# Layer 1 of a two-layer graph kernel: where X W is computed, the order of the loop head, and the broadcast of the weights

## The chip, the cores and the metric

The kernel runs on one core of a Trainium2 chip, in float32 throughout. The metric is the device time of one execution in microseconds (us); the runs shown are summed up by their median. A profile comes from one execution of its own, and its times are counted from that execution's first instruction.

## The reference, cut to what matters

There are N = 2708 nodes with 128 features; `adj` is a 2708 x 2708 matrix of zeros and ones. Layer 0 mixes neighbours and normalizes. Layer 1 is the part that the change is about:

```python
XW = X @ W                                  # 2708 x 128
s_col = XW @ a[0, :128]
s_row = XW @ a[0, 128:]
den = exp(leaky_relu(s_row[:, None] + s_col[None, :], 0.01))
num = A @ den
att = where(num != 0, den / num, 0)
H = A @ (att @ XW)
x = layernorm(X + H)
```

## The kernel before

**How layer 1 is computed.** exp(leaky(r + c)) is one of two exponentials, by the sign of r + c. So the kernel sorts the nodes into 24 groups of at most 126 by their row score and by their column score. A running sum over the groups then gives `num` with one matmul for each group and strip, where the plain way takes a product over all nodes. For this it needs the sorted order as tables of row numbers, and it gathers the rows of `adj_t` (its columns sorted by row score) and of XW (sorted by column score) with indirect DMAs.

**Stages, in order of time.**

1. Attention of layer 0, up to about 217 us.
2. Diffusion of layer 0 (lines 865 to 925). Six strips of 512 nodes (the last has 148), each 44 matmul instructions into `dif_acc`. After strip s come its normalized rows, turned (`x1_in_sbuf`, line 807, into tile `x1_t`), its scores (`scores`, `tally`, `picked`), and in strips 0 to 3 also X W of the strip (`projected`, line 848: four blocks, eight matmul instructions into `xw_ps`), copied by VectorE (line 887) and stored to the DRAM tensor `xw_d` through ScalarE's DMA queue (`store_xw`, line 857).
3. From line 897 on, the order on each engine is written out by hand: `mm`, `dve`, `act` and `gps` pin every instruction behind the one traced before it on the same engine (line 172). Strips 4 and 5 end here; their X W is done at lines 943 to 946, after the counts.
4. The look-up of interval ends (lines 984 to 1018). From the counts of nodes below each of 256 bounds the kernel follows, for 11 steps on VectorE, "the farthest bound that a group can reach" (line 988), and turns the ends into thresholds `thr`.
5. The tables (lines 1147 to 1241). Row scores (k) and column scores (j) are compared with `thr`, numbered, and placed with one-hot matmuls. The k tables give `k_no` (row numbers for `gather`), the j tables `j_no` (for `gather_xw`) and the sorted column scores `j_t`.
6. The loop over 24 groups (line 1340), a pipeline of three stages: step g multiplies group g (`multiply`, PE then a copy to `q`), divides group g-1 (`divide` on VectorE, `power` on ScalarE), weighs group g-2 with its XW rows (`weigh`, PE, into `m_acc`). ScalarE takes a logarithm and an exponential of each group, and loads a function table before each.
7. The last product with `adj_t` and the layer norm, from about 620 us.

**Fillers.** Sums over all rows that the groups start from (`tot`) are spread over stages 3 to 5 as jobs. An "e" job loads 128 rows of `adj_t` (768 KB, `first_strips`, line 691, a tile of pool `nat`) on SyncE's queue and sums them in eight small matmuls; a "k" job (`kept_strips`, line 707) sums rows that are in SBUF already, in twelve. `fill("eke")` puts three such jobs at this place of TensorE's order. There are 13 "e" and 22 "k" jobs left for `fill`.

**What the change and the prediction touch besides.** `att` (line 295, 22 blocks of 512 bytes per partition) is layer 0's attention term, last read by `mixed` in stage 3. Its pool `lp` is closed at line 950; the pools `tab` and `tmp` of stages 4 and 5 take over its memory. A new tile in memory taken over waits until the accesses to the old tile there have ended, DMAs among them. `ring[0]` is the memory of `x_sb`. `later_weights` (line 1258), called in step 0 of the loop, spreads the sorted column scores of groups 1 to 3 with matmuls, writes exp of all of them to the DRAM tensor `g_d`, and reads them back to all partitions with two broadcasting DMAs into `wt` (groups 4 to 7, then 8 to 23). `weights(g)` on ScalarE turns them into the weights of group g; it must be done before `multiply(g)`. `helped` (line 1291) names the two copies of step 0 that ScalarE makes instead of VectorE.

Of the kernel before, what the change touches and what calls it, by code (L numbers as in the profile page):

```python
# [45 lines left out]
def grouped(  # L46
# [602 lines left out]
    nat = pool("nat", 3, stack=l0)  # L649
# [157 lines left out]
    def x1_in_sbuf(s, tp):  # L807
        nb = blocks(s)
        x1_t = work2.tile([P, SW], F32, tag="x1_t", name="x1_t")
        dve(  # L810
            "tensor_copy", x1_t[:, : nb * P], tp[:, :nb, :].rearrange("p b i -> p (b i)")
        )
        return x1_t
# [34 lines left out]
    def projected(s, x1_t):  # L848
        pn = ps_mm.tile([P, SW // P, D], F32, tag="mm", name="xw_ps")
        for b in range(blocks(s)):  # L850
            mm(
                nc.tensor.matmul, pn[:, b, :], x1_t[:, ts(b, P)], w_sb,
                start=True, stop=True,
            )
        return pn

    def store_xw(s, xw, nb):
        nc.scalar.dma_start(
            xw_d[s * SW : s * SW + nb * P, :].rearrange("(b p) d -> p b d", p=P), xw
        )  # L860
# [4 lines left out]
    for s in range(NS - 2):  # L865
# [20 lines left out]
        xw = work2.tile([P, 4, D], F32, tag="xw", name="xw")  # L886
        nc.vector.tensor_copy(xw, projected(s, x1_t))
        store_xw(s, xw, nb)
# [24 lines left out]
    shared_row(s, row_s)  # L913
    fill("eke")
# [17 lines left out]
    shared_row(t, row_t)  # L932
    picked(t, col_t, sc_p)
# [4 lines left out]
    limited(s * 4, NB)  # L938
    picked(s, col_s, sc_p)
    act("activation", reach_b[64:], can[64:], AF.Copy, scale=-1.0, bias=Q + 1.0)  # L940
    dve("tensor_copy", reach_b[:64], reach_ps[:64, :Q])
    e2(s * 4, NB)
    xw = nat.tile([P, 6, D], F32, tag="xw_last", name="xw", bufs=1)
    act("copy", xw[:, :4, :], projected(s, x1_s))
    act("copy", xw[:, 4:, :], projected(t, x1_t)[:, :2, :])
    store_xw(s, xw, 6)
    fill("ekekek")
# [20 lines left out]
    vk = tmp.tile([P, NB], F32, name="vk")  # L968
    dve("scalar_tensor_tensor", vk, sr_p, -1.0, pad, ALU.mult, ALU.add)
    vj = tmp.tile([P, NB], F32, name="vj")  # L970
    dve("tensor_tensor", vj, sc_p, pad, ALU.add)
    back = tab.tile([P, NB], F32, name="back")
    dve("tensor_tensor", back, live, e2_p, ALU.mult)
# [13 lines left out]
    dve("tensor_copy", ends[64:, 0:1], reach_b[64:, Q - 1 :])  # L987
    for g in range(1, half_g):
        junk = tmp.tile([P, Q], F32, tag="more", name="junk")
        dve(  # L990
            "scalar_tensor_tensor", junk, bound_no, ends[:, g - 1 : g], reach_b,
            ALU.is_equal, ALU.mult, accum_out=ends[:, g : g + 1],
        )
    both = tmp.tile([P, NG - 1], F32, name="both")
    dve("tensor_scalar", both[:, : half_g - 1], ends[:, : half_g - 1], row0, None, ALU.mult)
    dve("tensor_scalar", both[:, half_g - 1 :], ends, half_on, None, ALU.mult)
    ends_ps = ps_x.tile([P, SW], F32, tag="ahead", name="ends_ps", bufs=2)
# [12 lines left out]
    fill("ekekk")  # L1010
# [90 lines left out]
    def table(name, onp, v, o, p0, between):  # L1101

        t = tmp.tile([P, 1, P], F32, name=f"{name}_t{v}")
# [27 lines left out]
    def gather_xw(g):  # L1131
# [5 lines left out]
            in_offset=bass.IndirectOffsetOnAxis(ap=j_no[:, g : g + 1], axis=0),  # L1137
# [3 lines left out]


    cs_p = tmp.tile([P, NB], F32, name="cs_p")
    dve("tensor_scalar", cs_p, sc_p, LIMIT, -LIMIT, ALU.min, ALU.max)
    dve("tensor_scalar", cs_p, cs_p, 1.0 - LEAK, None, ALU.mult)
# [6 lines left out]
    fill("kekekekek")  # L1152
# [4 lines left out]
    k_tab = table("k", k_onp, 0, *banks("x"), P - G, lambda: fill("kk"))  # L1157
    valued("k", 1, k_hot, low, 17)
    valued("j", 1, j_hot, cs_p, 0, 12)
    j_run, j_ahead, j_of = numbered("j", j_hot)  # L1160
    k_no = rows_of_table("k", k_tab, G)
    valued_by_dve("j", 0, j_hot, from_n)
    k_tab = table("k", k_onp, 1, *banks("x"), 0, lambda: fill("kkk"))
    valued("j", 1, j_hot, cs_p, 12)
    fill("k")
# [32 lines left out]
    gather(1)  # L1198
    wt = ring_p.tile([P, NG, P], F32, name="wt")
# [3 lines left out]
    carry_in(0, (0, 1), by_act)  # L1203

# [29 lines left out]
    j_tab = selected("j", j_t, [0, 1])  # L1234
    carry_in(0, (2, 3), by_dve)
    c_s = tab.tile([P, NG], F32, name="c_s")
    j_no = rows_of_table("j", j_tab, P)
    dve("tensor_copy", c_s, j_tab[:, 1, :])
    nc_s = tab.tile([P, NG], F32, name="nc_s")
    dve("tensor_scalar", nc_s, c_s, -1.0, None, ALU.mult)  # L1240
    carry_in(1, (0, 1), by_act)
    carry_in(1, (2, 3), by_dve)
    tots.close()
# [9 lines left out]
    gather_xw(0)  # L1253
    gather(2)
    gather_xw(1)
    gather(3)

    def later_weights():

        o = ps_num.tile([P, SW], F32, tag="num", name="c_ps")  # L1260
        for g in range(1, 4):
            spread_c(o[:, ts(g - 1, P)], g)
        mm(
            nc.tensor.matmul, o[:NG, 3 * P :], four[:, :NG], j_t[:, 1, :],
            start=True, stop=True,
        )
        g_r = tab.tile([P, P], F32, name="g_r")
        act("activation", g_r[:NG], o[:NG, 3 * P :], AF.Exp)
        nc.sync.dma_start(g_d, g_r[:NG, P - G :])
        act(  # L1270
            "activation", gb[:, 1:, :],
            o[:, : 3 * P].rearrange("p (g c) -> p g c", g=3)[:, :, P - G :], AF.Exp,
        )
        for g in range(1, 4):
            weights(g, gb[:, g, :])
        for g0, g1 in ((4, 8), (8, NG)):
            nc.sync.dma_start(
# [62 lines left out]
    for step in range(NG + LAG):  # L1340
# [17 lines left out]
        if g < NG:  # L1358
            for i0, i1 in parts_m:
                log(g, i0, i1)  # L1360
# [553 lines left out]
```

## Time and profile before

| what | value |
|---|---|
| runs shown | 739.69, 739.81, 743.85 us; median 739.81 us |
| the profiled execution's own time | 739.68 us |
| its span, first to last instruction | 737.9 us |
| mean granted TensorE clock | 0.982 of full speed |
| TensorE, VectorE, ScalarE, GpSimd busy | 708.7, 443.8, 419.5, 233.9 us |
| data moved by DMA | 179.89 MB, mean 244 GB/s |

The profiled execution takes 1.8 us more than its span; its time is 0.13 us from the median. Three kinds of answer are used below. A timeline lists instructions by start time with, in square brackets, how long the engine had been idle before and which instruction or DMA released it. A table of stretches gives each engine's busy time in a stretch with the number of its instructions, then the granted clock, the busy share of the DMA engines, and GB/s. The list of DMA issues gives the size of each and the time from issue to landing. PE is TensorE, PEld its weight loads, DVE VectorE, ACT ScalarE, POOL GpSimd, SP SyncE.

### The profile page before, as it was taken

The page shows a single profiled execution, that of the slowest core. Times are in us where ns is not written, and L with a number is a line of the kernel's source. Part 1 is how long each engine was busy: PE and PEld are TensorE (multiplying, and loading weights), DVE is VectorE, ACT ScalarE, POOL GpSimd, SP SyncE. Part 2 cuts the span into 40 slices and gives each one's busy share as a digit, 9 for nine tenths or more (in the row PEclk, how much of TensorE's full clock was granted, in tenths as well). Part 3 has the DMA queues.
Part 4 walks back from the last instruction along what each step waited for, and adds up shares of the span by engine and source line. Part 5 has one row for each costly group of instructions (what it writes and reads, how often), then busy time and mean ns, then how long its engine had stood idle before and what let it go on. Part 6 is the DMA issues. An engine that isn't in the chain of part 4 may idle for free. (4 is left out here: it accounts for less than half of the span.)

```text
span 737.9 us, 7958 instructions
## 1 busy us (share of the span) xinstructions
PE 708.7 (96%) x2639; PEld 358.8 (49%) x2639; DVE 443.8 (60%) x925; ACT 419.5 (57%) x601; POOL 233.9 (32%) x240
## 2 busy tenths in 40 slices
PE   7999999999999999999798899999999999999995
PEld 4454444545464444445565344444444446444444
DVE  5676857566541452344787879999999984103032
ACT  4757867778741121211176899999999994001000
POOL 5868788879841000000004222222222300000000
PEclk9999999999979999999989999999999999999999
DMA  8868999988999998731847994444444531999970
GB/s 287 314 226 300 325 326 338 336 316 299 301 365 400 364 395 301 288 143 33 286 143 251 230 222 149 167 173 171 165 158 155 165 133 42 298 311 309 313 228 24
DMA packets 69827, 179.89 MB, mean 244 GB/s; under 512 B 6798, under 2 KB 20914, under 8 KB 66754
## 3 DMA queue, kind: packets, MB, share of 16 engines
q1 hardware_dynamic: 57188, 133.32, 52.4%
q0 software_dynamic: 6336, 43.08, 17.7%
q10 hardware_dynamic: 6254, 2.90, 1.4%
q8 instruction: 23, 0.38, 0.2%
q14 instruction: 26, 0.21, 0.1%
HBM read 176.44 MB, written 2.84 MB: 243 GB/s over the span
## 5 line engine op out<-in xcount | busy, mean ns | idle before, releaser
L201 POOL TENSOR_TENSOR total<-total,p_t 128x512 f32<-128x512 f32 (+3 forms) x111 | 124.5, 1122 | 38.3 <-ACT p_t L195 32.8
L176 PE MATMUL m_acc<-q,xws 128*128 128x512 f32 x240 | 122.2, 597 | 0.0
L176 PE MATMUL num<-ring,wt 128*128 128x512 f32 x216 | 98.8, 550 | 4.4 <-DVE q L176 3.3
L190 DVE SCALAR_TENSOR_TENSOR p_t<-sim,gentle,piece 128x512 f32<-128x512 f32 (+1 forms) x111 | 72.2, 670 | 48.5 <-PE sim L185 37.8
L185 PE MATMUL att_acc<-p_t,x_sb 128*128 128x512 f32 (+1 forms) x228 | 97.6, 555 | 2.0 <-ACT p_t L195 1.8
L185 PE MATMUL dif_acc<-strip,x_sb 128*128 128x512 f32 x220 | 98.4, 594 | 0.0
L195 ACT ACTIVATE p_t<-p_t,shift 128x512 f32<-128x512 f32 (+1 forms) x111 | 69.4, 655 | 35.0 <-DVE p_t L190 29.6
L176 DVE SCALAR_TENSOR_TENSOR q<-sr_b,nc_s,q 128x1536 f32<-128x1536 f32 (+1 forms) x48 | 77.8, 1623 | 17.8 <-ACT q L176 17.6
L176 DVE COPY q<-num 128x512 f32<-128x512 f32 (+1 forms) x142 | 83.9, 612 | 4.4 <-PE num L176 4.2
L176 PEld LDWEIGHTS m_acc<-q,xws 128*128 128x128 f32 x240 | 45.9, 192 | 56.9 <-issue 56.7
L1451 PE MATMUL h_acc<-ring,m_sb 128*128 128x512 f32 x164 | 72.3, 593 | 0.0
L176 ACT ACTIVATE q<-q,head,rest 128x1536 f32<-128x1536 f32 (+1 forms) x48 | 70.2, 1508 | 1.2 <-DVE ring L176 0.9
L176 ACT ACT_TABLE_LOAD x52 | 66.7, 1283 | 3.8 <-issue 2.9
L176 PEld LDWEIGHTS num<-ring,wt 128*128 128x128 f32 x216 | 39.4, 191 | 49.2 <-issue 34.2
L176 ACT ACTIVATE q<-q,c_s 128x1536 f32<-128x1536 f32 (+1 forms) x48 | 62.9, 1355 | 0.4
L185 PEld LDWEIGHTS att_acc<-p_t,x_sb 128*128 128x128 f32 x228 | 40.9, 202 | 45.0 <-ACT p_t L195 25.0
L185 PEld LDWEIGHTS dif_acc<-strip,x_sb 128*128 128x128 f32 x220 | 40.5, 190 | 45.8 <-issue 45.8
L176 ACT ACTIVATE row<-row 128x1354 f32<-128x1354 f32 x44 | 58.2, 1323 | 7.5 <-DMA row<-in_adj 7.5
L1461 ACT COPY ht<-h_acc 128x512 f32<-128x512 f32 (+1 forms) x6 | 3.2, 535 | 91.3 <-PE h_acc L1451 91.2
L1466 DVE TENSOR_TENSOR hh<-rows,x 128x512 f32<-128x512 f32 (+1 forms) x6 | 3.8, 641 | 84.1 <-PE rows L1385 81.7
L176 POOL DMA_INDIRECT ring<-in_adj_t,k_no x18 | 21.1, 1170 | 100.3 <-PE num L176 97.2
L1451 PEld LDWEIGHTS h_acc<-ring,m_sb 128*128 128x128 f32 x164 | 30.8, 190 | 36.8 <-issue 36.8
(289 smaller groups left out, 907.8 us busy)
## 6 DMA issues: line engine op xcount, KB each, us to landing
row<-in_adj SPq DMA_DIRECT2D x44, 677.0 KB, 5.4
strip<-in_adj_t SPq DMA_DIRECT2D x10, 2816.0 KB, 19.3
piece<-in_adj_t SPq DMA_DIRECT2D x24, 1024.0 KB, 7.0
ring<-in_adj_t SPq DMA_DIRECT2D x20, 1024.0 KB, 5.0
nat<-in_adj_t SPq DMA_DIRECT2D x13, 768.0 KB, 4.5
x_sb<-in_adj_t SPq DMA_DIRECT2D x7, 1024.0 KB, 5.0
nat<-in_adj_t POOLq DMA_DIRECT2D x9, 768.0 KB, 9.8
piece<-in_adj_t SPq DMA_DIRECT2D x7, 512.0 KB, 6.6
```

The costliest lines, as they stand in the source:

```text
L176: latest[engine] = op(*args, **kwargs)
L185: op(*args, **kwargs)
L190: return getattr(nc.vector, op)(*args, **kwargs)
L195: return getattr(nc.scalar, op)(*args, **kwargs)
L201: getattr(nc.gpsimd, op)(*args, **kwargs)
L1451: nc.tensor.matmul(acc[:, : h1 - h0], m_sb[:, kb + b, :], a[:, b, h0:h1], start=(kb + b == 0), stop=(kb + b == NB - 1),)
L1461: nc.scalar.copy(ht[:, h0:h1], acc[:, : h1 - h0])
L1466: nc.vector.tensor_tensor(hh[:, b0 : b0 + n, :], rows[:, :n, :], x1[:, ib + b0 : ib + b0 + n, :], ALU.add)
```

## The change

It has seven parts.

1. **X W moves.** The four `projected` calls of strips 0 to 3, their VectorE copies and stores leave the diffusion. `x1_in_sbuf` now keeps the turned rows of every strip in `att` in place of a tile `x1_t`. After the counts, `project` makes X W of all six strips from there, ScalarE copies it back into the same place, and two DMAs store it (blocks 0 to 11 after strip 2, blocks 12 to 21 at the end).
2. **Order before the look-up.** `vk`, `vj`, `cs_p` and `back` are computed behind the 11 steps instead of before them; `limited` and `e2` of the last strips come after the third `project`. `shared_row(s, ...)` of strip 4 goes from before the second `tally` to behind strip 5's.
3. **Fillers in another order**, with "e" jobs earlier and "k" jobs later, and a fourth buffer for the pool `nat`. To have room, `junk` of the look-up is put into `x_sb`, the two tiles `k_t` share one place, and `x1_t`, `xw` and `xw_last` are gone.
4. **Tables.** `valued_by_dve("j", 0, ...)` comes before `k_no`; four "k" jobs stand before the j tables, where there was one.
5. **Before the loop.** `gather(2)` directly follows `gather(1)`. The four `carry_in` pairs come before the j tables' matmuls. What `later_weights` did with matmuls, exponentials, the write of `g_d` and the broadcast of groups 4 to 7 now comes ahead of the loop; the broadcast of groups 8 to 23 is written at the end of step 1.
6. **In step 0.** The selection of `j_no` and `c_s` (`numbers`) and the first two `gather_xw` come after the second multiply. `weights(1)`, `weights(2)` and the two halves of the logarithm are interleaved with the multiplies; ScalarE makes the copies of strips 1 and 4 instead of 1 and 3. `weights(3)` comes after step 1's logarithm.
7. **In step 2** `weigh(0, ...)` stands before the multiply of each strip instead of after it.

```diff
-    nat = pool("nat", 3, stack=l0)
+    nat = pool("nat", 4, stack=l0)
...
-        x1_t = work2.tile([P, SW], F32, tag="x1_t", name="x1_t")
+        x1_t = att[:, s * 4 : s * 4 + nb, :].rearrange("p b i -> p (b i)")
...
+    def project(s):
+        mine = att[:, s * 4 : s * 4 + blocks(s), :]
         pn = ps_mm.tile([P, SW // P, D], F32, tag="mm", name="xw_ps")
         for b in range(blocks(s)):
             mm(
+                nc.tensor.matmul, pn[:, b, :], mine[:, b, :], w_sb, start=True, stop=True
+            )
+        act("copy", mine, pn[:, : blocks(s), :])
...
-        xw = work2.tile([P, 4, D], F32, tag="xw", name="xw")
-        nc.vector.tensor_copy(xw, projected(s, x1_t))
-        store_xw(s, xw, nb)
...
-    shared_row(s, row_s)
-    fill("eke")
+    fill("eeke")
...
     shared_row(t, row_t)
+    shared_row(s, row_s)
...
-    limited(s * 4, NB)
+    act("activation", reach_b[64:], can[64:], AF.Copy, scale=-1.0, bias=Q + 1.0)
     picked(s, col_s, sc_p)
-    act("activation", reach_b[64:], can[64:], AF.Copy, scale=-1.0, bias=Q + 1.0)
     dve("tensor_copy", reach_b[:64], reach_ps[:64, :Q])
-    e2(s * 4, NB)
-    xw = nat.tile([P, 6, D], F32, tag="xw_last", name="xw", bufs=1)
-    act("copy", xw[:, :4, :], projected(s, x1_s))
-    act("copy", xw[:, 4:, :], projected(t, x1_t)[:, :2, :])
-    store_xw(s, xw, 6)
-    fill("ekekek")
+    for n in range(NS):
+        project(n)
+        if n == 2:
+            store_xw(0, 3)
+            limited(s * 4, NB)
+            e2(s * 4, NB)
+    store_xw(3, NS)
+    fill("e")
...
-    fill("ekekk")
+    fill("ekekek")
+    back = tab.tile([P, NB], F32, name="back")
+    dve("tensor_tensor", back, live, e2_p, ALU.mult)
...
-    fill("kekekekek")
+    fill("kkekkekke")
...
-    k_tab = table("k", k_onp, 0, *banks("x"), P - G, lambda: fill("kk"))
+    k_tab = table("k", k_onp, 0, *banks("x"), P - G, lambda: fill("k"))
...
+    valued_by_dve("j", 0, j_hot, from_n)
     k_no = rows_of_table("k", k_tab, G)
-    valued_by_dve("j", 0, j_hot, from_n)
-    k_tab = table("k", k_onp, 1, *banks("x"), 0, lambda: fill("kkk"))
+    k_tab = table("k", k_onp, 1, *banks("x"), 0, lambda: fill("kekk"))
     valued("j", 1, j_hot, cs_p, 12)
-    fill("k")
+    fill("kkkk")
...
+    def spread_out_weights(g0, g1):
+        nc.sync.dma_start(
+            wt[:, g0:g1, P - G :],
+            g_d[g0:g1, :].unsqueeze(0).to_broadcast([P, g1 - g0, G]),
+        )
+
+    spread_out_weights(4, 8)
...
+            if first == 0 and s < NS - 1:
+                weigh(first, *item)
             if g < NG:
                 multiply(g, *item)
                 if (g, s) == (0, 1):
-                    later_weights()
+                    j_no.append(numbers())
+                    gather_xw(0)
+                    gather(3)
+                    gather_xw(1)
+                if (g, s) == (0, 4):
+                    weights(2, gb[:, 2, :])
                 if item[2] == half or s == NS - 1:
                     carry(g, *parts_m[s // 3])
+                    if g == 0:
+                        if s < 3:
+                            weights(1, gb[:, 1, :])
+                        log(0, *parts_m[s // 3])
...
+        if step == 1:
+            spread_out_weights(8, NG)
```

## The prediction

> **What bounds the kernel now.** I read the timeline of each stage first, then the table of stretches for the clock, then the list of DMA issues. The sum is made against the profiled execution's 739.68 us (span 737.9 us and 1.78 us around it), which is 0.13 us below the median of the runs.
>
> In the diffusion (217 to 344 us) the timeline shows TensorE without a pause: whatever is issued there moves the end. X W of strip 0 stands between two runs of `dif_acc`:
>
> ```profile
> 250.48 1.05 PE L185 MATMUL xw_ps<-w_sb,x_t 128*128 128x128 f32 x8
> 251.37 1.02 PE L185 MATMUL dif_acc<-strip,x_sb 128*128 128x512 f32 x2
> ```
>
> Its slot is the distance of the starts, 251.37 - 250.48 = 0.89 us.
>
> Between 347 and 395 us VectorE carries a chain, with waits of its own. The brackets name what ended each:
>
> ```profile
> 348.58 0.75 DVE L176 TENSOR_SCALAR_CACHE_REDUCE junk<-sb_ps,ntheta 128x512 f32<-128x512 f32 x1 [0.85 <-ACT sr_b L176]
> ...
> 360.00 0.18 DVE L176 TENSOR_TENSOR back<-live,e_p 128x22 f32<-128x22 f32 x1 [1.52 <-ACT e_p L176]
> ...
> 369.40 0.17 DVE L176 COPY thr<-thr_ps 128x11 f32<-128x11 f32 x1 [1.60 <-PE thr_ps L176]
> ...
> 374.37 0.70 DVE L176 TENSOR_TENSOR k_run<-k_run,ahead 128x528 f32<-128x528 f32 x1 [0.84 <-PE ahead L176]
> ```
>
> TensorE is nearly idle during the look-up and pays for it. These stretches (TensorE's busy time first, then five columns with the clock after them) are the 3.4 us before each of two drops, and the drops:
>
> ```profile
> 362.60:366.00 3.40, 0.34 (x11) 0.15 (x2) 3.19 (x13) 0.00 (x0) 0.00 (x0) 1.00 1.03 363
> 366.00:372.80 6.80, 6.15 (x46) 3.88 (x50) 4.28 (x14) 1.38 (x6) 0.00 (x0) 0.50 0.61 214
> 386.50:389.90 3.40, 1.76 (x39) 1.27 (x33) 3.30 (x3) 3.39 (x16) 1.60 (x1) 1.00 0.87 293
> 389.90:393.30 3.40, 3.40 (x74) 3.34 (x68) 1.62 (x5) 0.29 (x1) 0.54 (x1) 0.50 0.76 268
> ```
>
> In the group loop ScalarE has no gap once it runs: its weights of successive groups start at 434.71 and 443.57, 8.86 us for a step. So a delay at the head is kept to the end. In step 2 it does stand still:
>
> ```profile
> 421.84 1.36 ACT L176 ACTIVATE q<-q,head,rest 128x1172 f32<-128x1172 f32 x1 [0.89 <-DVE ring L176]
> 425.85 0.49 ACT L176 ACTIVATE wt<-wt,kt 128x126 f32<-128x126 f32 x1 [2.65 <-DMA wt<-g_d]
> ```
>
> The list of issues has the DMA behind that wait, and the stores of X W:
>
> ```profile
> wt<-g_d SPq DMA_DIRECT2D x1, 1008.0 KB, 37.3
> ...
> xw_d<-xw ACTq DMA_DIRECT2D x4, 256.0 KB, 7.6
> ...
> xw_d<-xw ACTq DMA_DIRECT2D x1, 384.0 KB, 8.3
> ...
> wt<-g_d SPq DMA_DIRECT2D x1, 252.0 KB, 20.3
> ```
>
> **The change, part by part.** Clock times from here on are those of the profile before, so that shifts can be read against its rows.
>
> *Diffusion.* Four slots of 0.89 us go: **-3.56 us**. Strips 3 and 4 are issued 29 us before TensorE reads them and take 19.3 us at the median, so the loads stay hidden. VectorE's copies (4 x 0.69 us) lay beside TensorE and bring nothing.
>
> *Second tally.* It waited 0.85 us for ScalarE's copy of the same bank, which now comes later. The added "e" job costs TensorE about 0.6 us ahead of `x_ps` (two jobs start at 346.61 and 347.28, 0.67 us apart), which falls into its idle 1.34 us. Of the 0.85 I take **-0.7 us**.
>
> *Look-up.* `back` waited 1.52 us for `e_p`. Without it the steps start when ScalarE's half of `reach_b` is there, 358.45, and end at 364.9, where they ended at 366.50: 1.6 us earlier. Beside them TensorE now has X W of 22 blocks. Twelve instructions took 1.50 us, so 44 take 5.5 us, from 358.0. They are paced by ScalarE: copies of 0.585 us, two PSUM buffers, and in the middle the store's issue of 0.36 us, the table load of 1.28 and the exponential of 0.21. Strip 5 then ends at 364.9, the "e" job at 365.5, so `ends_ps` starts 0.6 us after VectorE is ready. But the clock should now stand at full: twelve small matmuls that took 1.20 us at 367.18 took 0.68 at 359.97, and `thr` follows `ends_ps` by about 1.6 us instead of 2.75. `thr` is there at 367.1 where it was at 369.4: 2.3 us.
>
> *Tables.* The three "e" and three "k" jobs behind `thr_ps` take 3.4 us warm (five took 4.6 us cold), so `ahead` is ready at 371.1 and the wait of 0.84 goes: 3.2 us. `valued_by_dve` (1.14 us) fills the wait of 1.30 us that `k_no` had, so the j chain gains another 0.9: its one-hots end at 386.7, not at 390.88. The j matmuls, 4.5 us at half clock, follow at full clock behind four "k" jobs of about 0.5 us, which end at 386.1. The first `num` starts near 390.5 where it started at 395.32: **4.8 us** at best. The earlier "e" jobs find their loads landed, because the fourth buffer takes one more into the idle queue at 315 to 347 us; `gather(0)` is issued at 381 and lands before 388.
>
> *What that gives back.* `j_gt` and the placing tiles lie in the memory of `att`, which the second store still reads. VectorE meets `j_gt` at 370.4; queued behind it are `k_run` and with it both tables. The store (640 KB) is issued at 365.9. Alone, the quickest store landed 2.3 us after issue for 256 KB; beside three loads 384 KB took 8.3. The wait lies between 0 (landing by 370.4) and 3.8 us (landing after 8.3, at 374.2). It has two or three 768 KB loads beside it, fewer than the row of 8.3 had queued ahead, so I take landing at 371.7 with **+0.6 us** after the slack behind `k_of` (0.7 us). Here the Trainium skill, "DMA: Bandwidth & Descriptors", section "Issuing engines are not separate DMA queues", speaks against the change: a store from ScalarE's queue shares the same 16 engines with SyncE's loads, and only the issue is saved. By the rule at its strictest, with the four later loads (3.1 MB at about 310 GB/s, 10 us) all served before it, the wait is 8 us, and the sum below becomes 737; by the rows, where 512-byte packets came through in 8.3 us between three loads, it is under 3.8. I take the rows.
>
> So the first multiply gains 4.8 - 0.6 - 0.3 (`num` may wait for ScalarE's reading of `c_ps` in the same bank, 0 to 0.75 us) = **-3.9 us**.
>
> *Clock.* "TensorE: Matmul & The Clock Gate", section "Why this matters for your kernels", says that gaps under about 3 us between bursts are safe. The rows disagree: the stretch from 386.5 had 1.76 us of work in 3.40 and no gap over 1.6 us (387.94 to 389.54), and the clock still halved. By the rule, the 1.4 us that X W waits for ScalarE's table load is harmless. By the row it is close: a stretch with that gap holds 2.0 of 3.4 us. I take the clock as kept, and carry the other outcome as a rival.
>
> *Loop head.* In order of ScalarE: copy, weights, table load, then the first half of the logarithm as soon as three strips are copied. VectorE's `carry` ends 5.0 us after the first multiply; the logarithm started 6.8 us after it before. But the second half now stands behind a copy of 0.58 and weights of 0.42 us, and the exponential behind VectorE's `divide`: its last part ends 14.3 us after the first multiply, before 14.0. Nothing gained, 0.3 us lost. The gain is in the broadcast. `g_r` is made at the first multiply, not 3.0 us after it, so the DMA lands 3 to 4 us earlier against the loop: the 2.65 us wait goes, or shrinks to 0.5. The wait of 0.89 us for `carry` may stay. Bounds: 0 (the gathers, two of them now earlier, hold the small packets as long as they did) to -3.5; I take **-2.2 us**, with the 0.3 in it. `weigh(0)` ahead of the multiplies in step 2 needs the exponential at 12.4 us and XW rows gathered from 3.5 us on, which take 6.0 us: nothing.
>
> *Sum.* -3.56 - 0.7 - 3.9 - 2.2 = -10.36; 739.68 - 10.36 = **729.3 us**, 729.4 beside the median. The loop of 8.86 us a step and the last product are only shifted.
>
> **The rivals.**
>
> *The clock falls again* (0.16). For it: the row of 1.76 us. At half clock the six fillers take 6 us, not 3.4, `thr` is 0.6 us later, and `ahead` comes near 373.6: the tables gain about 0.7 us instead of 3.9. 739.68 - 3.56 - 0.7 - 0.7 - 2.2 = **732.5 us**.
>
> *The broadcast is no earlier and the store holds `j_gt`* (0.13). For it: 20.3 us with gathers beside it, and gathers are as many as before. Head 0 and 2.5 us more of wait: 739.68 - 3.56 - 0.7 - 1.4 = **734.0 us**.
>
> *Slower: the second store starves* (0.10). Its 512-byte packets are like the 504-byte packets of the broadcasts, which landed after 20.3 and 37.3 us beside large transfers. If the store takes 20.3 us it lands at 386.2, `j_gt` stands still for 15.8 us, and VectorE's whole order with it; less 0.6 taken already: 729.3 + 15.2 = **744.5 us**. It decides from a landing 16 us after issue. Against it: five stores took at most 8.3 us.
>
> **How the numbers follow.** The forecast of 729.3 has a chance of 0.61, with a range of its own of 727 to 731.5; the rivals 0.16, 0.13 and 0.10. About 1%, 7.4 us, is what a measurement of this kernel can tell from no change; that line is 732.4. Below it lie the forecast and, of the first rival, which is at the line, about a third: 0.66. Over 1% slower is only the third: 0.10. Same: 0.24. From 726.5 to 735.0 us lie the forecast with its bounds and the first two rivals; 2 in 10 are left for the third and for tails.
>
> **What would show it.** `dif_acc` of strip 4 ending 3.5 us earlier; no wait of VectorE for `e_p`; `thr` about 6.5 us earlier on the clock; no drop of the clock between `ends_ps` and the j tables; `j_gt` with a wait for a DMA under 1.5 us; the first `num` near 387; ScalarE's wait for `wt` under 0.6 us. It is wrong if `j_gt` waits for the store by over 4 us, if the clock halves in the look-up, or if the diffusion does not shorten.

## The result and the profile after

The changed kernel takes **729.49 us** at the median of four runs (729.12 to 731.68), beside 739.75 us for the kernel before (739.14 to 743.85, four runs): a ratio of 0.9857, 95% interval 0.9824 to 0.9889. The profiled execution took 729.28 us, its span is 727.5 us, and the mean granted clock 0.989.

The attention stage, which the change does not touch, ends between 215.6 and 221.4 us in the profiles of this study. So stages are compared by the distance between two marks, and the total from the start of the diffusion on. Each column is read from one execution:

| stretch (us) | before | after | difference | forecast |
|---|---|---|---|---|
| start of the diffusion to the last strip's first `dif_acc` | 119.89 | 116.32 | -3.57 | -3.56 |
| from there to the counts `ct` | 15.89 | 14.98 | -0.91 | -0.7 |
| `ct` to the first `num` | 42.19 | 39.00 | -3.19 | -3.9 |
| first `num` to the logarithm of step 3 | 36.56 | 32.82 | -3.74 | -2.2 |
| that logarithm to the last one | 176.72 | 176.73 | +0.01 | 0 |
| last logarithm to the end | 129.28 | 129.56 | +0.28 | 0 |
| from the start of the diffusion to the end | 520.54 | 509.41 | -11.13 | -10.36 |

The spans differ by 10.4 us, since the diffusion of the profile after happens to start 0.73 us later. The first four rows, which are the terms that the prediction priced, come to -11.41.

*Diffusion*, the timeline of TensorE: sixteen matmul instructions of a strip follow each other with nothing between them.

```profile
249.49 7.03 PE L185 MATMUL dif_acc<-strip,x_sb 128*128 128x512 f32 x16
```

*Look-up and tables*, TensorE and then VectorE. X W runs beside VectorE's steps; the 0.84 us is its wait for ScalarE, which loads a table between two copies, and `ends_ps` starts as soon as VectorE's `both` is there (360.98 us):

```profile
354.11 4.72 PE L176 MATMUL xw_ps<-w_sb,att 128*128 128x128 f32 x40
359.67 0.71 PE L176 MATMUL xw_ps<-w_sb,att 128*128 128x128 f32 x4 [0.84 <-ACT att L176]
360.31 0.85 PE L176 MATMUL tot<-nat,e_w 128*32 128x384 f32 x8
361.09 0.40 PE L176 MATMUL ends_ps<-both,ones 128*128 128x23 f32 x2
```

```profile
362.72 0.17 DVE L176 COPY thr<-thr_ps 128x11 f32<-128x11 f32 x1 [0.59 <-PE thr_ps L176]
...
365.94 0.19 DVE L176 COPY k_of<-k_run 128x24 f32<-128x24 f32 x1
367.25 0.73 DVE L176 TENSOR_TENSOR j_gt<-vj,thr 128x550 f32<-128x550 f32 x1 [1.13 <-ACT k_ons L176]
367.90 0.70 DVE L176 TENSOR_TENSOR k_run<-k_run,ahead 128x528 f32<-128x528 f32 x1
```

The wait for `thr` shrank from 1.60 to 0.59 us. `j_gt` has a new wait of 1.13 us. The profile names ScalarE's `k_ons`, but these instructions had begun at 364.71 and run on without a break to 373.97; the experiments show that it is the store.

The table of stretches has the clock at full (1.00) where it had halved:

```profile
358.40:361.80 3.40, 2.56 (x27) 1.58 (x28) 3.14 (x18) 2.07 (x5) 1.20 (x5) 1.00 0.73 233
...
382.40:385.80 3.40, 2.77 (x95) 2.50 (x85) 2.43 (x8) 1.91 (x6) 2.15 (x2) 1.00 0.59 183
385.80:389.20 3.40, 2.51 (x12) 1.65 (x13) 1.07 (x3) 1.52 (x5) 0.00 (x0) 1.00 0.99 366
```

*Before the first multiply*, TensorE, first in the kernel before and then in the changed one. `c_ps` now stands ahead of `num`, which waits for ScalarE's reading of it, and `gb_ps` waits for `j_t`:

```profile
389.54 4.48 PE L176 MATMUL tab_ps<-j_onp,j_ons 128*32 128x128 f32 x88 [1.59 <-DVE j_onp L176]
393.95 0.49 PE L176 MATMUL gb_ps<-j_t,four 128*128 128x128 f32 x2
394.41 0.63 PE L176 MATMUL j_sel<-four,j_t 128*128 128x24 f32 x4
395.32 1.99 PE L176 MATMUL num<-x_sb,wt 128*128 128x512 f32 x4 [0.29 <-ACT wt L176]
```

```profile
382.36 2.81 PE L176 MATMUL tab_ps<-j_onp,j_ons 128*32 128x128 f32 x88
385.97 0.49 PE L176 MATMUL gb_ps<-j_t,four 128*128 128x128 f32 x2 [0.80 <-ACT j_t L176]
386.39 1.26 PE L176 MATMUL c_ps<-j_t,four 128*24 128x128 f32 x8
388.37 1.98 PE L176 MATMUL num<-x_sb,wt 128*128 128x512 f32 x4 [0.72 <-ACT gb L176]
```

ScalarE copies `j_t` late because two of the `carry_in` copies, which the change moved forward, stand ahead of it:

```profile
384.83 0.80 ACT L176 COPY x_sb<-tot 2x293 f32<-2x293 f32 x2 [1.21 <-DVE x_sb L176]
385.65 0.27 ACT L176 COPY j_t<-tab_ps 128x128 f32<-128x128 f32 x1
```

*Loop head*, ScalarE in step 2: neither the stall of 0.89 us inside the logarithm nor the 2.65 us before the weights of group 4 (at 415.17) is left. The list of issues has the broadcast behind it, which took 20.3 us before, and the first store:

```profile
412.34 2.92 ACT L176 ACTIVATE q<-q,head,rest 128x1536 f32<-128x1536 f32 x2
415.17 0.48 ACT L176 ACTIVATE wt<-wt,kt 128x126 f32<-128x126 f32 x1
```

```profile
xw_d<-att ACTq DMA_DIRECT2D x1, 768.0 KB, 4.1
...
wt<-g_d SPq DMA_DIRECT2D x1, 252.0 KB, 13.9
```

### The profile page after: what moved, and what is told of

It is laid out like the page before. It is cut to its first block, busy times and chain, and to the rows that moved or that the text cites. A ratio compares the mean times of both kernels' runs of the same rounds, so it can differ in the third digit from the quotient of the medians.

```text
span 727.5 us, 7944 instructions
## 1 busy us (share of the span) xinstructions
PE 702.9 (97%) x2639; PEld 354.5 (49%) x2639; DVE 440.1 (61%) x921; ACT 421.0 (58%) x605; POOL 233.2 (32%) x240
```

## The experiments

Intervals of the ratios are about 0.3 to 0.5% to each side, 2 to 4 us, which is as much as most single parts are worth. So the ratio says where a kernel stands, and the marks in the traces say which part did it. The marks of a kernel come from one execution, which can lie off its median: by +2.8 us of 740.2 for the kernel before with the broadcast early, and by +1.6 us of 736.6 for the changed kernel with `gather(2)` in the loop. The loop's head scatters most, so a difference of 1 us there in a single row proves little. In the table, "dif" is the first stretch of the table above, "tables" runs from `ct` to the first `num`, "head" from there to the logarithm of step 3, "rest" from the start of the diffusion to the end.

| kernel | ratio to before, interval | dif | tables | head | rest |
|---|---|---|---|---|---|
| before | 1 | 119.89 | 42.19 | 36.56 | 520.54 |
| after | 0.9857 (0.9824 to 0.9889) | 116.32 | 39.00 | 32.82 | 509.41 |
| X W in the diffusion | 0.9876 (0.9844 to 0.9908) | 119.82 | 40.16 | 32.84 | 513.90 |
| the same, TensorE filled | 0.9880 (0.9839 to 0.9922) | 119.81 | 37.83 | 34.52 | 513.34 |
| before, TensorE filled | 0.9949 (0.9912 to 0.9985) | 119.89 | 41.76 | 35.32 | 519.77 |
| write of `g_d` late | 0.9848 (0.9777 to 0.9919) | 116.32 | 39.11 | 32.82 | 509.47 |
| `j_gt` behind `k_onp` | 0.9843 (0.9800 to 0.9887) | 118.42 | 39.34 | 34.56 | 513.35 |
| before, broadcast early | 0.9988 (0.9963 to 1.0014) | 119.89 | 42.64 | 36.08 | 521.65 |
| before, `gather(2)` early | 1.0012 (0.9982 to 1.0042) | 119.89 | 40.95 | 35.34 | 518.10 |
| before, both early | 1.0014 (0.9981 to 1.0047) | 119.89 | 42.88 | 37.57 | 522.28 |
| after, `gather(2)` in the loop | 0.9910 (0.9863 to 0.9956) | 116.32 | 39.47 | 39.77 | 517.16 |
| after, logarithm at the end | 0.9862 (0.9820 to 0.9904) | 116.32 | 40.55 | 32.65 | 510.53 |
| after, `c_ps` in another bank | 0.9869 (0.9834 to 0.9903) | 116.32 | 39.43 | 32.72 | 509.53 |
| the same, store in two | 0.9866 (0.9828 to 0.9903) | 116.32 | 38.86 | 32.85 | 509.41 |

**X W back in the diffusion.** The changed kernel with X W of strips 0 to 3 at its old place, stored strip by strip, and with that of strips 4 and 5 stored together.

```diff
     (in the loop over strips 0 to 3, behind e2)
+        project(s)
+        store_xw(s, s + 1)
...
-    for n in range(NS):
-        project(n)
-        if n == 2:
-            store_xw(0, 3)
-            limited(s * 4, NB)
-            e2(s * 4, NB)
-    store_xw(3, NS)
+    project(s)
+    limited(s * 4, NB)
+    e2(s * 4, NB)
+    project(t)
+    store_xw(s, NS)
```

> The changed kernel with X W of strips 0 to 3 put back into the diffusion (each strip's eight matmul instructions, its copy by ScalarE and its own store), all else as changed. Theory (X W costs its slot of 0.89 us in the diffusion, and in the look-up it also keeps the clock up): the diffusion is 3.56 us longer; TensorE is then idle for about 4 us of the look-up, the clock falls to half, thr comes 0.6 us later and the six fillers behind it hold ahead for about 2.5 us. 729.5 + 3.6 + 3 = 736. Rival (the fill has no share, VectorE sets the stage): 733. Second rival (the diffusion was not bound by TensorE): 729.5 to 732.5.

Measured: the diffusion is 3.50 us longer, four slots of 0.88. One slot stands in the timeline of this kernel (253.55 to 254.44):

```profile
253.55 1.05 PE L185 MATMUL xw_ps<-w_sb,att 128*128 128x128 f32 x8
254.44 4.03 PE L185 MATMUL dif_acc<-strip,x_sb 128*128 128x512 f32 x9
```

`j_gt` waits 0.03 us, not 1.13, with a store of 384 KB, issued earlier, in the place of the one of 640 KB. But TensorE, without X W in the look-up, is given half the clock from 365.4 us on, and `thr` is 14.51 us behind `ct` instead of 13.35. The table of stretches of this kernel:

```profile
362.00:365.40 3.40, 0.25 (x4) 0.00 (x0) 3.19 (x13) 1.42 (x3) 0.92 (x5) 1.00 0.71 220
365.40:372.20 6.80, 5.22 (x42) 3.68 (x46) 4.70 (x20) 0.49 (x3) 0.00 (x0) 0.50 0.30 93
```

**The same, with idle matmuls in the place of X W.** Sixteen matmuls that nothing reads keep TensorE busy in the look-up; nothing is left out.

```diff
     store_xw(s, NS)
+    idle_ps = ps_mm.tile([P, SW], F32, tag="mm", name="idle_ps")
+    for _ in range(16):
+        mm(nc.tensor.matmul, idle_ps[:, :P], w_sb, ident, start=True, stop=True)
```

> The kernel of the run before with 16 matmuls whose output nobody reads (128 x 128, 32 instructions, about 3.5 to 4 us) in the look-up, where the changed kernel has X W of strips 0 to 3. They leave nothing out of the computation. Theory (slot and clock are two separate shares): the clock stays full, and only the four slots of 0.89 us remain: 729.5 + 3.6 = 733.1. Rival (what counts is that the stores and copies moved, not the clock): 736, like the run before.

Measured: the clock stays full in the look-up, and the first `num` comes 37.83 us after `ct`, 2.33 us sooner than without the filling. That is the price of the clock alone. Against this kernel the changed one loses 1.17 us in the tables, and its wait at `j_gt` is 1.13: X W in the look-up brings 2.33 us by the clock and pays 1.17 with its store. In the loop's first step this kernel lost 1.7 us again, because the clock halved there:

```profile
388.20:391.60 3.40, 1.88 (x13) 1.30 (x12) 1.21 (x3) 2.18 (x7) 0.25 (x1) 1.00 0.86 319
391.60:395.00 3.40, 3.40 (x5) 1.34 (x6) 0.69 (x1) 0.00 (x0) 0.00 (x0) 0.50 0.89 268
```

The changed kernel has the same instructions in the same order there, with the same two waits of 0.80 and 0.72 us, and kept its clock. In the look-up and the tables none of the seven traces that have X W in the look-up shows a halving.

**The kernel before, filled in the same way.** Only idle matmuls are added, eight behind the fillers that precede the look-up's end and three ahead of the j tables.

```diff
+    idle_ps = ps_mm.tile([P, SW], F32, tag="mm", name="idle_ps")
+    for _ in range(8):
+        mm(nc.tensor.matmul, idle_ps[:, : 2 * P], w_sb,
+           ones.unsqueeze(1).to_broadcast([P, 2, P]), start=True, stop=True)
...  (and, ahead of the j tables, three of the same form)
```

> The kernel before with matmuls whose output nobody reads: eight (128 x 256, about 3.4 us) after the fillers that precede the look-up's end, and three (1.3 us) ahead of the j tables. Nothing else is changed. Theory (half clock cost TensorE's part of the chain): thr 0.6 us earlier, the wait of 0.84 us for ahead gone, the j tables 1.5 us earlier: 739.7 - 2.5 = 737.2, no drop of the clock between 360 and 395 us. Rival (the waits were order, not clock): 739.7, though the clock is full.

Measured: the clock is full from 360 to 395 us, but the first `num` comes only 0.43 us sooner. TensorE's order stood still for fillers' loads ahead of the idle matmuls, which so began late, and `ends_ps` waited behind them (VectorE's `both` was there at 367.04):

```profile
365.04 3.72 PE L176 MATMUL idle_ps<-ones,w_sb 128*128 128x256 f32 x16
368.60 0.30 PE L176 MATMUL ends_ps<-both,ones 128*128 128x23 f32 x2
```

Behind `thr` the fillers waited for their loads again, by 1.68 and 1.31 us, and VectorE waited 3.12 us for `k_sel`, not 1.30. What the full clock gave back, 1.48 us between the j one-hots and the first `num`, did not make up for more. So this kernel does not show what the clock alone is worth: the work that kept it up has to be over in time.

Its loop has no edit, and yet its head is 1.24 us shorter than that of the kernel before: the broadcast landed 29.25 us after the first `num`, not 30.50, and a longer halving of the clock held step 2 back, so only 0.06 us of the wait for the weights was left.

**The write of `g_d` late.** The changed kernel, with the write and the broadcast behind step 0's first half, where `g_d` was written before.

```diff
-    nc.sync.dma_start(g_d, g_r[:NG, P - G :])
...
-    spread_out_weights(4, 8)
...
+                            act("copy", g_late[:NG], g_r[:NG])
+                            nc.sync.dma_start(g_d, g_late[:NG, P - G :])
+                            spread_out_weights(4, 8)
```

> The changed kernel with the write of g_d and both broadcasts held back behind weights(1) of step 0 by a copy of g_r on ScalarE (0.25 us), so that they are issued about 3.5 us later against the first multiply, as in the kernel before. Theory (the wait for wt went because the broadcast is issued earlier): weights(4) has 5.5 us to spare in the changed kernel; 3.5 us later alone would be covered, but the packets then meet the gathers as before (20.3 us to land, not 13.9), which is 9.9 us later in all: a wait of 3 to 4.5 us, 733. Rival (the landing is set by the gathers that were put elsewhere, not by its issue): landing near 14 us, no wait, 729.8.

Measured: no difference (head 32.82). SyncE's timeline, of this kernel and of the changed one:

```profile
391.13 0.38 SPq L1364 DMA_DIRECT2D g_d<-g_late  x1
395.17 1.40 SPq L1254 DMA_DIRECT2D wt<-g_d  x2
```

```profile
387.98 0.38 SPq L1248 DMA_DIRECT2D g_d<-g_r  x1
395.76 1.11 SPq L1255 DMA_DIRECT2D wt<-g_d  x2
```

Measured from the first `num`, which comes 0.45 us earlier in this trace, the write is 3.59 us later, and the broadcast behind it, which must wait for it to land, goes out 0.15 us earlier: from the write to the broadcast it took 4.0 us instead of 7.8. The broadcast then landed after 14.0 us, as against 13.9. So an earlier `g_r` is not why the wait for the weights went.

Up to `j_gt` this kernel is the changed one, and here the profile names the store as what `j_gt` waits for:

```profile
366.81 0.73 DVE L176 TENSOR_TENSOR j_gt<-vj,thr 128x550 f32<-128x550 f32 x1 [1.23 <-DMA xw_d<-att]
```

**`j_gt` moved behind `k_onp`** on VectorE, so that nothing of the k tables is queued behind its wait.

```diff
-    j_gt = beyond("j", vj)
     k_own = chosen("k", k_hot, k_run, k_ahead)
     k_onp = placed("k", k_own)
+    j_gt = beyond("j", vj)
```

> The changed kernel with j_gt computed behind the placing of k instead of ahead of it, so that VectorE meets the memory of the stored X W about 1.2 us later. Theory (j_gt's wait of 1.13 us is for the second store of X W, and lies on the path): the wait goes, the k tables come 1.1 to 1.8 us earlier, the first num about 1.1 us earlier, 1.1 us off the total. Rival (the k tables wait for ScalarE's k_ons, which end at the same instant, and everything behind is bound by that): under 0.3 us.

Measured: the wait is gone and `k_run` comes 3.90 us after `thr`, not 5.18. But the first `num` is no earlier against `ct` (39.34): the j chain has to make up for `j_gt` later, so its one-hots end only 0.45 us earlier, and TensorE's j tables show pauses that no releaser explains:

```profile
381.39 1.69 PE L176 MATMUL tab_ps<-j_onp,j_ons 128*32 128x128 f32 x51
383.25 0.30 PE L176 MATMUL tab_ps<-j_onp,j_ons 128*32 128x128 f32 x2 [0.17 <-issue]
383.95 0.42 PE L176 MATMUL tab_ps<-j_onp,j_ons 128*32 128x128 f32 x4 [0.40 <-issue]
384.69 1.29 PE L176 MATMUL tab_ps<-j_onp,j_ons 128*32 128x128 f32 x31 [0.32 <-issue]
```

Its diffusion and head are not comparable with the changed kernel's: TensorE waited 1.87 us for one strip, and the broadcast landed after 21.9 us, which brought back a wait of 1.49 us before the weights.

**The kernel before with the broadcast early.** `c_ps`, `g_r`, the write of `g_d` and the broadcasts stand ahead of the loop; the rest is as before.

```diff
+    c_ps = ps_x.tile([P, SW], F32, tag="sel", name="c_ps", bufs=2)
...
+    nc.sync.dma_start(g_d, g_r[:NG, P - G :])
...
-        o = ps_num.tile([P, SW], F32, tag="num", name="c_ps")
...
-        nc.sync.dma_start(g_d, g_r[:NG, P - G :])
```

> The kernel before, with the matmuls and exponentials of the later weights, the write of g_d and both broadcasts issued ahead of the loop, about 3 us earlier; order of the gathers as before. Theory (after the run with the late broadcast: what else is in the queues sets the landing, not the issue): the write of g_d takes longer, the broadcast goes out little earlier and lands after about 20 us, and the wait for wt stays at 1.5 us or more: under 1 us gained. Rival (the prediction's: an earlier issue takes the wait away): the wait of 2.65 us goes, 2.5 us gained.

Measured: the broadcast is issued at 400.65 us and lands after 14.3; no wait for the weights is left. Yet the head gains only 0.48 us, since `gather(2)` is late instead. TensorE in step 2:

```profile
413.98 2.05 PE L176 MATMUL num<-ring,wt 128*128 128x512 f32 x2 [3.25 <-DMA ring<-in_adj_t,k_no]
```

**The kernel before with `gather(2)` early**, directly behind `gather(1)`.

```diff
     gather(1)
+    gather(2)
...
     gather_xw(0)
-    gather(2)
     gather_xw(1)
```

> The kernel before with the one edit that gather(2) is issued directly behind gather(1), before the j tables, instead of in the loop's head. Theory (a gather of 1.4 MB less beside the write of g_d and the broadcast is what let them land early): g_d lands 2 to 3 us sooner, the broadcast takes about 14 us instead of 20, the wait for wt goes: 2.5 us gained. Rival (the early issue did it): the wait stays near 2.65 us, nothing gained.

Measured: the head is 1.22 us shorter; the broadcast lands after 18.6 us, and the wait before the weights is 1.43 us, not 2.65. That is no more than the head of the filled kernel before gained without any edit there (1.24), and the broadcast landed at the same distance from the first `num` (29.28 us). So this trace does not show a gain. (Its tables are 1.24 us shorter because the clock halved later, at 372.4 us, 15.2 us behind `ct`, and `thr` was just there.)

**The changed kernel with `gather(2)` back in the loop.**

```diff
     gather(1)
-    gather(2)
...
                     gather_xw(0)
-                    gather(3)
+                    gather(2)
                     gather_xw(1)
+                    gather(3)
```

> The changed kernel with gather(2) put back between the two gathers of X W rows in step 0. Theory (the place of gather(2) decides): the broadcast lands after about 20 us, at 27 to 28 us after the first num, and weights(4), wanted at 26.8 us, wait 0.5 to 2 us; the second gather also comes late for step 2. 1 to 2 us lost. Rival (the early issue decides): no wait, nothing lost.

Measured: the broadcast, with no large gather just ahead of it, lands after 6.1 us, the quickest of all. The head is 6.95 us longer for that, because the gather, issued 0.6 us behind the broadcast, is late. This execution is the slowest of the kernel's six (731.96 to 738.21 us); by the ratios the loss is about 4 us:

```profile
409.73 2.04 PE L176 MATMUL num<-ring,wt 128*128 128x512 f32 x2 [5.36 <-DMA ring<-in_adj_t,k_no]
```

**The kernel before with both early.** If the two transfers only hid each other, this should have had most of the head's gain.

```diff
     gather(1)
+    gather(2)
...
+    c_ps = ps_x.tile([P, SW], F32, tag="sel", name="c_ps", bufs=2)
...
+    nc.sync.dma_start(g_d, g_r[:NG, P - G :])
...
     gather_xw(0)
-    gather(2)
     gather_xw(1)
```

> The kernel before with both transfers of the loop head early: gather(2) right behind gather(1), and c_ps, g_r, the write of g_d and the broadcasts ahead of the loop; ScalarE's order in step 0 is as before. Alone they brought 1.22 and 0.48 us from the first multiply to step 3's logarithm. Theory (the head is bounded by transfers, each of the two hides the other): no wait for wt and none for gather(2), 36.56 - 2.65 = 33.9 us or less. Rival (the gains only add): 34.9.

Measured: 37.57 us, worse than the kernel before; both theories miss. `g_d` was written at 396.83 us, but its broadcast went out only at 405.07, and landed 23.1 us later. Where the two theories expected a gain of 1.7 us or more, 1.0 was lost. ScalarE in step 2:

```profile
422.41 1.36 ACT L176 ACTIVATE q<-q,head,rest 128x1172 f32<-128x1172 f32 x1 [0.89 <-DVE ring L176]
428.23 0.49 ACT L176 ACTIVATE wt<-wt,kt 128x126 f32<-128x126 f32 x1 [4.45 <-DMA wt<-g_d]
```

The head start of the two is not enough. In this kernel `gather(3)` and `gather(4)` are issued 3.3 and 5.5 us after the first multiply, both ahead of the broadcast; in the changed one at 4.2 and 7.65 us, the second behind it, because `numbers` and the gathers follow the second multiply.

**The changed kernel with the logarithm at the end of step 0**, and ScalarE's copies for strips 1 and 3 as before.

```diff
-    helped = {(0, 1), (0, 4)}
+    helped = {(0, 1), (0, 3)}
...
-                        log(0, *parts_m[s // 3])
...
-            if g > 0:
-                for i0, i1 in parts_m:
-                    log(g, i0, i1)
+            for i0, i1 in parts_m:
+                log(g, i0, i1)
```

> The changed kernel with ScalarE's order of step 0 nearer to before: both halves of the logarithm after the last copy, copies of strips 1 and 3 as before; transfers as changed. Theory (the early first half of the logarithm is worth something of its own, since the first logarithm began 5.1 instead of 6.8 us after the first multiply): step 3's logarithm 1.0 to 1.6 us later, 33.8 to 34.4 instead of 32.82. Rival, as the prediction has it (the order gains nothing, its last part ends no earlier): 32.5 to 32.9.

Measured: the head is 32.65 us. ScalarE's first logarithm starts 6.47 us after the first multiply instead of 5.10, and the next one 8.47 us after it instead of 10.01; what was won by starting early is given back at once, in the changed kernel, by the copy, the weights and 0.43 us of waiting between its halves. So the order of ScalarE in step 0 gains nothing; this one trace has it at a loss of 0.17 us. (Its tables are 1.55 us longer: 1.3 in the j tables, which show pauses as those of `j_gt` behind `k_onp`, and 0.22 more at `j_gt`.)

**`c_ps` in another PSUM bank, alone and with the store in two.** The last two kernels look for what is left.

```diff
-    c_ps = ps_x.tile([P, SW], F32, tag="ahead", name="c_ps", bufs=2)
+    c_ps = ps_x.tile([P, SW], F32, tag="sel", name="c_ps", bufs=2)
```

and, in the second of them also,

```diff
             e2(s * 4, NB)
-    store_xw(3, NS)
+        if n == 4:
+            store_xw(3, 5)
+    store_xw(5, NS)
```

> The changed kernel with c_ps in the other pair of PSUM buffers (tag sel). Theory: num's 0.72 us wait at the first multiply is for ScalarE reading c_ps in a bank that num takes over; in another bank it goes: first num 0.7 us nearer to the end of the j tables, span less the start of the diffusion 508.7 instead of 509.4. Rival: num takes over that bank as well, or waits for something else that ends as late: 509.4, no change.

> c_ps in the other buffers, and the second store of X W cut in two: strips 3 and 4 stored after strip 4, strip 5 after itself. Theory (the 1.13 us before j_gt is the second store landing, and it is late because it is issued late and large): most of it leaves about 1 us earlier, j_gt waits 0.3 us or less, 0.8 us gained on top of the first experiment of this call. Rival (the store waits behind the loads that share the engines, whatever its size): j_gt still waits 1.1 us, and one more issue on ScalarE costs up to 0.4 us.

Measured: with the other bank the wait of 0.72 us is gone; the first `num` follows `j_t` after 2.01 us, not 2.72. But the j tables took 4.08 us instead of 3.29 from their first matmul to `j_t`, with unexplained pauses of about 0.3 us, and started 0.36 later, so the total is the same (509.53). TensorE of this kernel:

```profile
385.39 0.41 PE L176 MATMUL tab_ps<-j_onp,j_ons 128*32 128x128 f32 x4 [0.29 <-issue]
386.13 0.44 PE L176 MATMUL tab_ps<-j_onp,j_ons 128*32 128x128 f32 x5 [0.33 <-issue]
...
388.51 1.26 PE L176 MATMUL c_ps<-j_t,four 128*24 128x128 f32 x8
389.61 1.88 PE L176 MATMUL num<-x_sb,wt 128*128 128x512 f32 x4
```

With the store in two, `j_gt` waits about half as long, and the profile names the store:

```profile
368.79 0.73 DVE L176 TENSOR_TENSOR j_gt<-vj,thr 128x550 f32<-128x550 f32 x1 [0.52 <-DMA xw_d<-att]
```

From `thr` to `k_run` it takes 4.56 us instead of 5.18; in the end 509.41, as the changed kernel. Neither beats it.

## Why the prediction was right, and where its steps were not

**Diffusion and tally: right.** Four slots of 0.89 us were taken away and 3.57 us went; X W put back costs 3.50. The wait of 0.85 us in the second tally went whole (0.91): the added "e" job fell into idle time, as the prediction had it, with less of a loss than the 0.15 allowed.

**Look-up: right in kind, 0.6 us too cautious.** From `ct` to `thr` it gained 2.91 us, where 2.3 were forecast. X W and the "e" job were expected to hold `ends_ps` for 0.6 us; it started 0.11 us after `both`. What the full clock brings is shown by the pair of kernels with and without filling: 2.33 us from `ct` to the first `num`.

**The store: the mechanism right, the size low.** `j_gt` waits 1.13 us; the wait goes when the large store goes (0.03), halves when most of the store leaves earlier (0.52), and is put down to the store by name in the traces with the write of `g_d` late (1.23) and with `gather(2)` in the loop (1.26). Taken were 0.6 after slack, from bounds of 0 and 3.8. The strictest reading of the prediction, a store behind all loads, would have given a wait of 8 us and 737 us in all. The first store, 768 KB, landed after 4.1 us between the loads. That fits what the Trainium skill says in "DMA: Bandwidth & Descriptors" ("Issuing engines are not separate DMA queues"): DMAs from different engines share the 16 DMA engines and interleave. It does not say that one waits for all the others, so the 8 us were not the skill's.

**From the j one-hots to the first `num`: the step that failed.** The prediction has the one-hots end at 386.7 us on the clock of before and the first `num` at 390.5, "4.8 us at best", less 0.6 for the store and 0.3 for the bank. Put on that clock (3.76 us, the shift of `ct`, added) the one-hots ended at 386.70, as forecast without the store: 2.91 us gained up to `thr`, 0.20 lost from there to `k_run`, 1.46 gained behind it. The look-up and the j chain paid for the store. But from there to the first `num` it took 5.43 us, where 4.1 were forecast and 4.44 had been before. The rows in the section on the result show three things that the sum had wrong. The eight matmuls of `c_ps`, 1.26 us, stand ahead of `num` and were left out. TensorE stands still for 0.80 us before `gb_ps`, since the copy of `j_t` is queued behind the `carry_in` copies on ScalarE; before, ScalarE had been waiting for the j tables and TensorE went on at once. And the wait for the bank is 0.72 us and not 0.3. Against that, `j_sel` (0.63 us) has left the stretch. So from `ct` to the first `num` the change brought 3.19 us for 3.9. The 1.26 us of `c_ps` are work moved out of the loop's head, where they are part of that term's gain. The bank wait could be taken away, though in that kernel other pauses ate what it gave.

**Loop head: the size low by 1.5 us, and the reason given was wrong.** The prediction expected the broadcast 3 to 4 us earlier because "`g_r` is made at the first multiply". Measured from the first `num`, the broadcast was issued after 10.23 us and landed after 30.5 before, and was issued after 7.39 and landed after 21.3 us in the changed kernel; it was asked for at 27.9 and 26.8. Only 2.8 us of the 9.2 come from the issue, and not from `g_r`: written 3.6 us later it made no difference. The rest is a quicker landing. The row of the kernel before, beside that of the changed one shown with the late write:

```profile
405.55 1.24 SPq L1277 DMA_DIRECT2D wt<-g_d  x2
```

Of the head's 3.74 us, 2.65 are the wait for the broadcast. The other 1.1 us is the stall inside step 2's logarithm ("may stay", says the prediction): in the step from logarithm 2 to 3, less the wait for the weights, the kernel before and its three variants with earlier transfers took 9.86 to 9.96 us and the changed kernel 8.85. The broadcast's date and `gather(2)`'s are no part of that. A rival is the clock, which halves in step 2 in every trace of the order before. But it halves there also in the changed kernel with `j_gt` behind `k_onp` and with the store in two (from 401.4 and 403.4 us), and these have no such stall. What is left is the place of `weigh(0)` in step 2. TensorE's row of the kernel before has an idle stretch before the first multiply of that step, which in the changed kernel `weigh(0)` fills, with 0.20 us of waiting left:

```profile
409.86 1.60 PE L176 MATMUL num<-ring,wt 128*128 128x512 f32 x2 [1.06 <-DVE q L176]
```

```profile
401.69 1.02 PE L176 MATMUL m_acc<-q,xws 128*128 128x512 f32 x2
402.92 1.12 PE L176 MATMUL num<-ring,wt 128*128 128x512 f32 x2 [0.20 <-DVE q L176]
```

By elimination that is the likely cause; it was not tried alone. ScalarE's order in step 0, priced at "nothing gained, 0.3 us lost", was right: putting half of it back made the head 0.17 us shorter.

How much of the 3.74 us would come again? Six of the eight traces with the changed kernel's order of transfers have a head of 32.65 to 32.85 us and two of 34.5; the order before, with no edit in the loop, has 36.56 and 35.32. So there is a gain, of 1 to 4 us by these traces; the 3.74 us of one pair are partly chance.

What makes the broadcast land sooner is **not settled**. Each of the two transfers alone changed the head of the kernel before by no more than it scatters (0.5 and 1.2 us), both together lost 1.0, and taking `gather(2)`'s head start from the changed kernel cost 6.95 in its trace. What the kernel with both still lacks is the later issue of the next gathers (part 6 of the change); that was not run alone. The order of the broadcast and `gather(4)` is not the reason: with `c_ps` in another bank `gather(4)` was issued 0.1 and 0.4 us ahead of the broadcast, which landed after 12.6 and 14.5 us, and in the two traces where it came 0.7 and 1.1 us behind, the broadcast took longest, 19.9 and 21.9 us. Over the eight traces the landing took 12.6 to 21.9 us. "In two parts" the broadcast is in the code alone: the two issues follow each other on SyncE at 395.76 and 396.22 us, since its queue waits for nothing else.

**The rivals.** The clock did not fall in the changed kernel, but the rival was real: without X W there it fell in the same stretch. The second, a broadcast that is no earlier and 2.5 us more of wait for the store, is excluded by the head's gain and the 1.13 us. The third rival, the starving store, is excluded by the 1.13 us. And the number 729.3 is close to 729.5 partly by chance: the steps forecast came to 1.05 us more than forecast (0.2 in the tally, 1.54 in the head, -0.7 in the tables), and a later start of the diffusion took 0.73 back.

## What to carry to other kernels

Work that fills an engine's idle stretch pays twice if it keeps the clock up (here 3.57 us from the place it leaves and 2.33 from the place it goes to), and costs once if its store's source is memory that a later stage takes over (1.13 us). When several transfers share the same few microseconds, date each against the instruction that needs it: moving one ahead made another late (3.25 us of waiting for `gather(2)`, 4.45 for the broadcast), and only the whole order gained clearly. When work is moved ahead of a critical instruction, put its own busy time into the sum (`c_ps`, 1.26 us), and what then queues behind it on its engine (`j_t`, 0.80 us), before asking about its waits.

## What the runs showed of the hardware

- **The clock.** In the kernel before the halvings began at 366.0, 389.9 and 410.4 us, 23.9 and 20.5 apart, seven and six times 3.41 us. In every trace with more than one, the starts from the diffusion on are whole multiples of 3.413 us apart; where in the program they fall differs from one execution to the next. Cut into windows in step with its own halvings, from 230 to 640 us, the fourteen traces have 17 halvings, each behind a window with at most 1.89 us of TensorE's work in 3.41; no window with more than 1.90 us was followed by one. Five windows of 1.4 to 1.9 us passed, so the share of work is not all of it. The longest pause decides less: 13 of the 17 windows have none over 1.73 us, and that of the filled variant, shown above, none over 0.80. The Trainium skill's "TensorE: Matmul & The Clock Gate" has a free-running activity window of about 3.4 us ("What's actually happening"), which fits. Its advice to avoid gaps over about 3 us ("Why this matters for your kernels") does not cover these 13. It also follows that the same instructions can keep the clock in one execution and lose it in another, as at the first `num` here.
- **Small packets among large ones.** 252 KB in rows of 504 bytes landed after 6.1 us in the one kernel that had no large gather just ahead of it, and after 12.6 to 23.1 us in the others. The write of `g_d`, 12 KB, held the broadcast behind it for 2.5 to 8.2 us.
- **Pauses without a releaser.** Four variants of the changed kernel show three pauses of 0.2 to 0.4 us in TensorE's j tables, and one a single pause; they begin within a few instructions behind the 48 of the first twelve blocks, and for two of them the profile names a copy of ScalarE. In the four it is 4.6 us from the first j matmul to the end of the last, where the changed kernel takes 2.8 and has no pause, though in one of them (the logarithm at the end) TensorE's instructions up to that place are the same. The changed kernel's wait of 0.80 us for `j_t` is gone in these four, so about 0.9 us is lost. The cause is open.
